# Four fused attention layers: layer 1 interleaved by batches, two result places in the heads, and a projection by seven products

## The chip, the cores and the metric

The kernel runs on one core of one Trainium2 chip. The metric is device time in microseconds of one execution, as the median of several runs; lower is better. All data are float32. The engines are named as in the profile: PE (TensorE, matmuls; PEld is its weight loads), DVE (VectorE), ACT (ScalarE), POOL (GpSimd) and SP (SyncE, which here only issues transfers and reads one flag).

## The reference, cut to what matters

Two images of 512 channels with 32 x 32 pixels pass through four layers, each of which adds to its input. Layer 0 is an attention with sampled keys and a small network for its position bias, followed by an MLP of 512 to 2048 to 512 channels. The change doesn't touch it. Layer 1 is a linear attention, layers 2 and 3 are group norm and full attention with 8 heads over 1024 positions:

```
# layer 1, n = 1024 positions, Q and K of 64 channels, V of 512
Q, K = Q / |Q|, K / |K|                       # over channels
tailor = 1 / (n + Q^T (sum_n K + eps))
x = x + gamma * (sum_n V + (V K^T) Q) * tailor

# layers 2 and 3
h = group_norm(x)
q, k, v = split(w_qkv h + b_qkv)              # 8 heads of 64 channels
a = softmax(q^T k / 8) v
x = x + (w_proj a + b_proj)                   # w_proj: 512 x 512
```

## The kernel before

The image x stays in SBUF for the whole run: `self.xs[b][t]` holds batch b, channels 128 t to 128 t + 127, as 128 partitions x 1024 positions. `CT` is 4, the number of channel tiles, `HF` is 512, half of the positions, and `DH` is 64. Weights come from DRAM by transfers on SP. The kernel is written in a framework that orders each engine's instructions by its own estimate, except inside `manual_schedule(engines=...)`: there the named engines run in the order of the text. Tiles come from pools; a tile whose buffer is still in use waits for the last reader of it. PSUM, where matmuls write, is given out in the same way.

**Layer 1** (`layer1`, L814 to L963). Queries and keys are made with positions on partitions (L844), x is transposed (L859), and norms give `qn` and `kn` (L867 to L873). Then for each batch: the sum of the keys on all partitions (`kb`, L883), x times keys (`m1`, 32 calls, L889), the key sum as a column (`s`, L900), the divisors folded into `qn` on DVE (L906 to L914), and `m`, the product with the value weights (L922), which becomes `mat` (L924). After both batches `qn` is transposed (L932), and the results `w` (L945) are added to x: for batch 0 by DVE out of PSUM (L950), for batch 1 by an ACT copy `ws` and a POOL addition (L956, L957). Only this last loop has a written order, on PE and DVE. It also makes the channel means of batch 0 for the group norm of layer 2 (`channel_means`, L1201, L1202; `group_means`, L1208 to L1219), and `norm_first` normalises the first block (`xn`).

**Queries, keys and values** of layers 2 and 3 (`queries_keys_values`) are products of 2 x 2 blocks by the scheme of seven products: `SEVEN` says for P1 to P7 which left and which right operand each multiplies, out of four blocks and three sums on either side. `left_side` has POOL make the left sums (`left_sums`, L658 to L661), `right_sums` has DVE make the right ones (L665 to L668). The MLP of layer 0 uses the same scheme.

**The heads** (`heads_bounded`) go over 16 units, unit (b, p, h): batch, pair of heads, half of the queries. A unit has eight steps n, one for each 128 keys. `score` puts 128 x 1024 logits into PSUM (L1276) and ACT takes their exp, `e` (L1280). `value` multiplies `e` with v into the unit's place `o` (L1305). The sum of the eight `e` is made by POOL (`some`, of n = 0, 1, 3, 5, L1285 and L1287) and DVE (`sum`, L1290, L1292, joined in L1294). `divide` spreads the sum over the partitions with a matmul `d` (L1322) and divides: L1327, the reciprocal L1328, L1330, L1331. The order on PE is written out: score i, then value i - 2, except that the first two values of a unit are put off to its fourth step; the division of a unit stands in the fifth step of the next one. Scores have two places in PSUM; `o` and `d` have one each:

```python
            ps_s = self.pool(ctx, f"b{k}_ps_s", 2, psum=True)
            ps_o = self.pool(ctx, f"b{k}_ps_o", 1, psum=True)
```

When a unit is done, ACT copies one half of `o` (L1314) and DVE adds the other (L1315); the result replaces the queries in `data[b][0]`.

**The projection** (`project_block`, L628) has for each batch and each of four output tiles eight calls of 128 x 128 by 128 x 512, then two DVE instructions that add bias and x (L637), and in layer 3 two stores (L639). In layer 2 one `channel_means` of layer 3 stands behind each of blocks 1 to 4, `group_means` behind blocks 5 and 6. Its weights are four tiles of their own, loaded as the heads begin (L977).

`attention` puts this together: a flag from the largest logits decides between `heads_bounded` and `heads_general`; with these inputs it is the former. While the flag is read, SP issues the loads of the next layer's weights (`meanwhile`).

Of the kernel before, what the change touches and what calls it, by code (L numbers as in the profile page):

```python
# [11 lines left out]
F32 = mybir.dt.float32  # L12
# [6 lines left out]
P = 128  # L19
# [33 lines left out]
class Net:  # L53
# [569 lines left out]
    def project_block(self, acc, att, w, bias: str, b: int, o: int, out):  # L623

        nc = self.nc
        for h in range(2):
            for t in range(CT):
                nc.tensor.matmul(  # L628
                    acc[:, h, :],
                    lhsT=w[t][:, o * P : (o + 1) * P],  # L630
                    rhs=att[t][:, h * HF : (h + 1) * HF],
                    start=(t == 0),
                    stop=(t == CT - 1),
                )
# [19 lines left out]
    def left_sums(eng, w, more):  # L654

        a11, a12, a21, a22 = (w[:, i] for i in range(4))
        s2, s3, s4 = (more[:, i] for i in range(3))
        eng.tensor_tensor(s3, a11, a21, ALU.subtract)  # L658
        eng.tensor_tensor(a21, a21, a22, ALU.add)
        eng.tensor_tensor(s2, a21, a11, ALU.subtract)  # L660
        eng.tensor_tensor(s4, a12, s2, ALU.subtract)  # L661
# [152 lines left out]
    def layer1(self, w, bias):  # L814
# [3 lines left out]
        with ExitStack() as ctx:  # L818
# [8 lines left out]
            xT, qk, qn, kn, q_at = [], [], [], [], []  # L827
# [49 lines left out]
            mats = []  # L877
            for b in range(B):


# [3 lines left out]
                kb = small.tile([P, DH + 1], F32, tag="kb", name=f"kbs{b}")  # L884
                nc.vector.tensor_scalar(kb, kb_ps, 1e-6, None, ALU.add)
                m1_ps = ps_m.tile([P, CT, DH + 1], F32, tag="m1", name=f"m1{b}")
                for t in range(CT):
# [8 lines left out]
                m1 = pool.tile([P, CT, DH + 1], F32, tag=f"m1{b}", name=f"m1s{b}")  # L896
                nc.scalar.copy(m1, m1_ps)
                s_ps = ps_m.tile([P, DH + 1], F32, tag="s", name=f"s{b}")
                for n in range(NB):
                    nc.tensor.matmul(  # L900
                        s_ps[0 : DH + 1, 0:1], lhsT=kn[b][:, n, :], rhs=ones[:, 0:1], start=(n == 0), stop=(n == NB - 1)
                    )
                ks = small.tile([DH + 1, 1], F32, tag="ks", name=f"ks{b}")
                nc.vector.tensor_copy(ks, s_ps[0 : DH + 1, 0:1])
                prod = pool.tile([P, NB, DH], F32, tag=f"prod{b}", name=f"prod{b}")
                nc.vector.tensor_tensor(  # L906
                    prod, qn[b][:, :, 0:DH], kb[:, 0:DH].unsqueeze(1).to_broadcast([P, NB, DH]), ALU.mult
                )
                d = small.tile([P, NB], F32, tag="d", name=f"d{b}")
                nc.vector.tensor_reduce(d, prod, AX.X, ALU.add)  # L910
                nc.vector.tensor_scalar(d, d, float(N), None, ALU.add)
                nc.vector.reciprocal(d, d)
                nc.vector.tensor_scalar(d, d, self.col("gamma1"), None, ALU.mult)
                nc.vector.tensor_tensor(  # L914
# [5 lines left out]
                m_ps = ps_m.tile([DH + 1, C], F32, tag="m1", name=f"m{b}")  # L920
                for t in range(CT):
                    nc.tensor.matmul(m_ps, lhsT=m1[:, t, :], rhs=w[:, t, 0:C], start=(t == 0), stop=(t == CT - 1))  # L922
                mat = pool.tile([DH + 1, C], F32, tag=f"mat{b}", name=f"mat{b}")
                nc.vector.scalar_tensor_tensor(mat, bias[0 : DH + 1, 0:C], ks, m_ps, ALU.mult, ALU.add)  # L924
                mats.append(mat)

            for b in range(B):
                for h in range(2):
                    cut = slice(h * HF, (h + 1) * HF)
# [4 lines left out]
                    nc.scalar.copy(qa, tr[0 : DH + 1, :])  # L934
                    q_at.append(qa)
            self.means_tiles(2, 0)
            self.first = {2: self.first_block(2, 0)}
            with self.tc.manual_schedule(engines={mybir.EngineType.PE, mybir.EngineType.DVE}):
                steps = self.group_means(2, 0, ps_m.tile([P, 2, CT], F32, tag="s", name="gm2"))
                for b in range(B):  # L940
# [638 lines left out]
```

## Time and profile before

| | us |
|---|---|
| median of 3 runs | 3430.6 (3429.81 to 3431.36) |
| the profiled execution | 3430.73 |
| its span, first to last instruction | 3428.9 |
| layer 1, from 2445.7 | 84.5 |
| layer 2: queries, keys, values / heads / projection | 150.1 / 241.2 / 58.4 |
| layer 3: queries, keys, values / heads / projection and end | 147.4 / 240.7 / 61.0 |

A group line of the profile has the line of the kernel, engine, operation, names of what is written and read, shape and count; then the busy time and the mean duration of one; then the engine's idle time ahead of it and what ended most of that. A timeline line begins with start and length in us, and may end with the idle time ahead and its releaser in brackets. Matmuls of float32 leave two records each, and the end of a record is modelled, so records overlap and a busy PE can hide short gaps. Stretches were cut at the first instructions of the stages.

### The profile page before, as it was taken

Reading aid. Unit: us, or ns where it says so; the run is one execution under the profiler, and the core shown is the slowest. Engines: PE = TensorE matmul, PEld = TensorE weight load, DVE = VectorE, ACT = ScalarE, POOL = GpSimd, SP = SyncE. Lnnn points to the kernel's source line nnn. Section 1 sums busy time; section 2 is a strip of 40 time slices with the busy share of each in tenths; the row PEclk is TensorE's granted clock in tenths of the full one; section 3 lists DMA queues with packets and bytes.
Section 4 is the critical chain, followed back from the end, with each engine's and each line's share of the span. In section 5 each row is a group of like instructions: output and inputs, shape, how many; then the busy total and the mean of one; then the engine's idle time right before and its main releaser. Section 6 shows DMA issues by size and latency. Waiting matters only on the chain.

```text
span 3428.9 us, 60151 instructions
## 1 busy us (share of the span) xinstructions
PE 3376.9 (98%) x25280; PEld 1243.1 (36%) x25280; DVE 2314.8 (68%) x2553; ACT 2020.2 (59%) x2102; POOL 2070.3 (60%) x1584
## 2 busy tenths in 40 slices
PE   6999999999999999999999999999999999999999
PEld 2333333333333333333333334444655433455333
DVE  6876777777776677777776664575556576555674
ACT  5887877877877688877877761111111566113661
POOL 4877777877877687878877873432324344234441
PEclk9999999999999999999999999999999999999999
DMA  5878777877877677878888861110000100000001
GB/s 152 158 150 158 158 150 153 160 151 152 160 148 146 119 158 148 167 146 156 161 165 157 161 155 63 49 49 25 1 1 6 45 2 1 1 0 13 1 1 51
DMA packets 103248, 342.65 MB, mean 100 GB/s; under 512 B 12720, under 2 KB 14384, under 8 KB 100144
## 3 DMA queue, kind: packets, MB, share of 16 engines
q0 software_dynamic: 73296, 266.90, 41.0%
q1 hardware_dynamic: 28656, 69.68, 7.1%
q8 instruction: 202, 3.31, 0.4%
q10 hardware_dynamic: 1008, 2.06, 0.2%
q14 instruction: 86, 0.70, 0.1%
HBM read 67.27 MB, written 4.46 MB: 21 GB/s over the span
## 4 chain that ended last, share of the span: by engine, by line
PE 86%; DVE 11%; ACT 1%; POOL 1%; issue 1%; DMA 0%; DVEq 0%; ACTq 0%
PE hp L515 50%; PE pb L628 3%; PE sim L547 3%; DVE r L1328 3%; PE o L1305 2%; DVE sum L1292 2%; PE s L1276 2%; PE qk20P L1071 1%; PE qk30P L1071 1%; PE m_0P L679 1%; PE qk21P L1071 1%; PE m_5P L679 1%; PE m_4P L679 1%; PE m_2P L679 1%; PE qk31P L1071 1%; PE m_6P L679 1%
## 5 line engine op out<-in xcount | busy, mean ns | idle before, releaser
L515 PE MATMUL hp<-h,w 128*32 128x512 f32 x16384 | 1822.1, 593 | 5.3 <-DVE h L484 3.6
L484 DVE CUSTOM_DVE_ANT_1 h<-tx,bank 128x1024 f32<-128x1024 f32 x1024 | 1179.9, 1215 | 276.6 <-PE hp L515 241.1
L520 ACT ACTIVATE h<-hp,magb 128x1024 f32<-128x1024 f32 x1024 | 1121.9, 1112 | 403.8 <-PE hp L515 398.8
L515 PEld LDWEIGHTS hp<-h,w 128*32 128x32 f32 x16384 | 530.4, 110 | 1221.4 <-issue 1154.3
L507 POOL DMA_DIRECT2D h<-h x509 | 451.8, 1022 | 410.4 <-ACT h L526 348.8
L533 POOL TENSOR_TENSOR h<-h,h 128x1024 f32<-128x1024 f32 x255 | 610.2, 2393 | 21.3
L531 POOL TENSOR_SCALAR h<-h,flip 128x1024 f32<-128x1024 f32 x256 | 446.9, 1746 | 0.9 <-ACT h L520 0.9
L1280 ACT ACTIVATE e<-s 128x1024 f32<-128x1024 f32 x256 | 258.4, 1024 | 177.6 <-PE s L1276 167.3
L522 ACT ACTIVATE h<-h,flip 128x1024 f32<-128x1024 f32 x256 | 291.4, 1138 | 0.0
L1305 PE MATMUL o<-e,v 64*64 64x512 f32 x2048 | 261.0, 592 | 6.9 <-DVE q L1315 6.9
L1276 PE MATMUL s<-q,k 64*64 64x512 f32 x2048 | 259.8, 589 | 2.6 <-DVE v L1109 1.8
L1287 POOL TENSOR_TENSOR some<-some,e 128x1024 f32<-128x1024 f32 x64 | 151.7, 2370 | 75.4 <-ACT e L1280 73.1
L1285 POOL TENSOR_TENSOR some<-e,e 128x1024 f32<-128x1024 f32 x32 | 75.6, 2364 | 190.9 <-DVE sum L1294 155.8
L524 POOL TENSOR_SCALAR h<-h,flip 128x1024 f32<-128x1024 f32 x128 | 144.5, 1129 | 47.9 <-ACT h L520 46.8
L526 ACT ACTIVATE h<-h,flip 128x1024 f32<-128x1024 f32 x128 | 145.6, 1138 | 0.0
L547 PE MATMUL sim<-h,ends 128*32 128x512 f32 x1024 | 142.5, 592 | 0.0
L1290 DVE TENSOR_TENSOR sum<-e,e 128x1024 f32<-128x1024 f32 x32 | 46.6, 1456 | 136.1 <-ACT e L1280 136.1
L1305 PEld LDWEIGHTS o<-e,v 64*64 64x64 f32 x2048 | 75.8, 133 | 157.4 <-issue 123.6
L1276 PEld LDWEIGHTS s<-q,k 64*64 64x64 f32 x2048 | 78.6, 133 | 143.4 <-issue 118.5
L738 ACT ACTIVATE mh<-mh,cols 128x512 f32<-128x512 f32 x64 | 46.2, 721 | 124.2 <-DVE mh L756 65.5
L658 POOL TENSOR_TENSOR mlp_w<-mlp_w 128x512 f32<-128x512 f32 x16 | 22.0, 1374 | 160.1 <-DMA mlp_w<-in_mlp_w 148.8
L1059 POOL TENSOR_TENSOR sq<-q 128x512 f32<-128x512 f32 x32 | 33.3, 1041 | 139.3 <-DVE q L1078 95.3
(463 smaller groups left out, 3278.6 us busy)
## 6 DMA issues: line engine op xcount, KB each, us to landing
h<-h POOLq DMA_DIRECT2D x509, 512.0 KB, 6.5
lb<-logs SPq DMA_DIRECT2D x63, 512.0 KB, 5.2
mlp_w<-in_mlp_w SPq DMA_DIRECT2D x16, 1024.0 KB, 4.9
x<-in_x SPq DMA_DIRECT2D x8, 512.0 KB, 9.4
qkw<-in_l_qk SPq DMA_DIRECT2D x2, 2048.0 KB, 8.2
out<-x SPq DMA_DIRECT2D x16, 256.0 KB, 2.1
vw<-in_l_v SPq DMA_DIRECT2D x2, 1024.0 KB, 7.6
proj<-in_l_proj SPq DMA_DIRECT2D x8, 256.0 KB, 5.0
```

Source lines behind the costliest of these rows:

```text
L484: self.nc.vector._custom_dve(TENSOR_ADD_SAT, out=h[:, k, :, :], in0=x[:, jj, 2 * r + k, :].unsqueeze(1).to_broadcast([P, H, W]), in1=y[:, ...
L507: nc.gpsimd.dma_start(to, what, accum_op=ALU.add)
L515: nc.tensor.matmul(hp[rows, cut], lhsT=self.l0w2[:, 32 * q : 32 * q + 32], rhs=h1[k][:, cut], start=True, stop=True)
L520: nc.scalar.activation(y, hp, AF.Relu, bias=self.magb[:, q : q + 1])
L522: nc.scalar.activation(ys[0], ys[0], AF.Copy, scale=self.flip[:, 0:1])
L531: nc.gpsimd.tensor_scalar(y, y, self.flip[:, 2:3], 1.0, ALU.mult, ALU.mult)
L533: (nc.vector if final else nc.gpsimd).tensor_tensor(y, y, ys[2], ALU.add)
L547: nc.tensor.matmul(sims[u][at : at + 32, :], lhsT=self.ends[:, 28 - 4 * o : 60 - 4 * o], rhs=z[jj][:, h * HF : (h + 1) * HF], start=(o == ...
L679: self.nc.tensor.matmul(acc[p], lhsT=w[:, a, k, p * P : (p + 1) * P], rhs=right(r, k), start=k == 0, stop=k == 1)
L1276: nc.tensor.matmul(s[halves[c], par, :], lhsT=ks[p][rows, at : at + DH], rhs=qs[p][rows, cut], start=True, stop=True)
L1280: nc.scalar.activation(e, s, AF.Exp, scale=DH**-0.5)
L1305: nc.tensor.matmul(o[halves[par], r, :], lhsT=v[n // 2][rows, n % 2, at : at + DH], rhs=e[rows, par, :], start=(n == 0), stop=(n == NB - 1),)
```

## The change

Four things are changed.

1. Layer 1. From the key sums on, the order is written out for PE, ACT and DVE. Batch 0 runs through to its `mat` first; its results are then made in turn with `m1` of batch 1 (two results, one channel mean, a quarter of `m1`), and the rest of batch 1 follows. `group_means` and `norm_first` stand among the results of batch 1.
2. Heads. PSUM now has four places, "a", "b", "even" and "odd". Scores take "a" and "b" in turn; `o` and then `d` of a unit take "even" or "odd" by its h. The values always follow two steps behind the scores. The order is written out for PE, DVE and POOL.
3. Projection. It becomes seven products of 256 x 256 by 256 x 512 for each batch. The left sums, and the right sums but three, are made by POOL during the heads of batch 1, two or three in the seventh step of a unit; the last three are made by DVE behind the last division. In P7 and P5 POOL adds to x.
4. Weights. The values' weights are loaded as the layer begins, and the projection's weights as one load into the same buffer, ahead of the reading of the flag. In memory they are stored by blocks.

```diff
     @staticmethod
     def left_sums(eng, w, more):
-        eng.tensor_tensor(s3, a11, a21, ALU.subtract)
...
+        for step in Net.left_steps(eng, w, more):
+            step()
...
     def layer1(self, w, bias):
...
+            engines = {getattr(mybir.EngineType, e) for e in ("PE", "Activation", "DVE")}
+            with self.tc.manual_schedule(engines=engines):
+                keys_sum(0)
+                for _ in divisors(0):
+                    pass
+                for _ in keys_x(0):
+                    pass
+                keys_column(0)
+                turned(0)
+                matrix(0)
+                keys_sum(1)
+                divided, summed = divisors(1), keys_x(1)
+                for t in range(CT):
+                    for h in range(2):
+                        result(0, h, t)
+                    self.channel_means(2, 0, t)
+                    next(summed)
+                    if t in (0, 2):
+                        next(divided, None)
+                next(summed, None)
+                keys_column(1)
+                turned(1)
+                matrix(1)
                 steps = self.group_means(2, 0, ps_m.tile([P, 2, CT], F32, tag="s", name="gm2"))
+                next(steps)
+                for h in range(2):
+                    for t in range(CT):
+                        result(1, h, t)
+                        if h == 0 and t == 2:
+                            next(steps, None)
+                        elif h == 1 and t == 1:
+                            self.norm_first(2)
...
     def queries_keys_values(self, k, wpool, weights, ones, data):
...
             with self.tc.manual_schedule(engines={mybir.EngineType.SP}):
-                got = meanwhile()
+                got = self.attention_weights(wpool, 3, "qk") if k == 2 else None
+                proj = self.attention_weights(wpool, k, "proj")
...
     def heads_bounded(self, k, ones, data, proj, out):
...
+            places = {x: self.pool(ctx, f"b{k}_ps_{x}", 1, psum=True) for x in ("a", "odd", "even", "b")}
...
-                third = unit is units[0] and n == 2
-                s = (ps_o if third else ps_s).tile([P, 2, HF], F32, tag="sd"[third], name=f"s{k}{b}{p}{h}{n}")
+                at = {0: "b", 1: "a", 2: "odd"}.get(n) if unit is units[0] else None
+                s = place(at or ("a", "b")[n % 2], f"s{k}{b}{p}{h}{n}")
...
-                    state["o"] = ps_o.tile([P, 2, HF], F32, tag="o", name=f"o{k}{b}{p}{h}")
+                    state["o"] = place(home(h), f"o{k}{b}{p}{h}")
...
-                d = ps_o.tile([P, 2, HF], F32, tag="d", name=f"d{k}{b}{p}{h}")
+                d = place(home(h), f"d{k}{b}{p}{h}")
...
+            for b in range(B):
+                att = data[b][0]
+                r = [[att[2 * (i // 2) + c][:, (i % 2) * HF : (i % 2 + 1) * HF] for c in range(2)] for i in range(4)]
+                if b == 0:
+                    t = [x.rearrange("p (c x) -> p c x", c=2) for x in data[0][1]]
+                else:
+                    t = data[0][2]
+                t1, t2, t3, t4 = ([x[:, c, :] for c in range(2)] for x in t)
+                right.append([r[0], t3, r[2], r[3], t1, t2, t4])
+                if b == 1:
+                    sums += self.left_steps(nc.gpsimd, proj, more)
+                    sums += [subtract(nc.gpsimd, t1[c], r[1][c], r[0][c]) for c in range(2)]
+                for c in range(2):
+                    eng, to = (nc.vector, late) if b == c == 1 else (nc.gpsimd, sums)
+                    if b == 0:
+                        to.append(subtract(eng, t1[c], r[1][c], r[0][c]))
+                    to.append(subtract(eng, t2[c], r[3][c], t1[c]))
+                    to.append(subtract(eng, t3[c], r[3][c], r[1][c]))
+                    to.append(subtract(eng, t4[c], r[2][c], t2[c]))
...
+                at = ("a", "b", "even", "a", "b", "even", "a") if b == 0 else ("odd", "even", "b", "odd", "even", "a", "b")
+                for which, spot in zip(("P1", "P3", "P2", "P6", "P7", "P5", "P4"), at):
...
+                        if which == "P1":
+                            nc.scalar.copy(u, got)
+                            add(vec, p, 0, got, True)
+                        elif which == "P3":
+                            add(vec, p, 1, got, True)
+                        elif which == "P2":
+                            add(vec, p, 0, got)
+                            store(p, 0)
+                        elif which == "P6":
+                            vec.tensor_tensor(u, got, u, ALU.add)
+                        elif which == "P7":
+                            u3 = u3s[:, p, :]
+                            vec.tensor_tensor(u3, got, u, ALU.add)
+                            add(pool, p, 3, u3)
+                            if p == 1:
+                                for q in range(2):
+                                    add(pool, q, 2, u3s[:, q, :])
+                        elif which == "P5":
+                            vec.tensor_tensor(u, got, u, ALU.add)
+                            add(pool, p, 1, u)
+                            store(p, 1)
+                            add(vec, p, 3, got, True)
+                            store(p, 3)
+                        else:
+                            add(vec, p, 2, got, True)
+                            store(p, 2)
+                    yield
...
-                for i in range(len(steps) + 5):
+                for i in range(len(steps) + 2):
                     if i < len(steps):
                         score(*steps[i])
-                    for j in ([], [i - 3, i - 2])[i % NB == 3] if i % NB in (2, 3) else [i - 2]:
...
+                    if i >= 2:
+                        value(*steps[i - 2])
                     if i % NB == 4 and NB < i < len(steps):
                         divide(steps[i - NB][0])
...
+                    if i % NB == 6 and i > len(steps) // 2 + NB:
+                        for _ in range(3 if i < len(steps) * 3 // 4 else 2):
+                            sums.pop(0)()
+                for n, _ in enumerate(project(0)):
+                    if n == 2:
+                        divide(units[-1])
+                        for do in late:
+                            do()
+                for n, _ in enumerate(project(1)):
+                    if k == 2:
+                        if n < 2:
+                            self.channel_means(3, 0, 2 * n)
+                            self.channel_means(3, 0, 2 * n + 1)
+                        elif n == 2:
+                            means = self.group_means(3, 0, place("a", "gm3"))
+                            next(means)
+                        elif n == 3:
+                            next(means, None)
+                            self.norm_first(3)
```

`add(eng, p, i, what)` adds a result to block i of x, `store` sends a block of the output in layer 3, and `left_steps` gives the four left sums one by one.

## The prediction

> **What bounds the kernel.** First the busy times and the chain of waits.
>
> ```profile
> span 3428.9 us, 60151 instructions
> PE 3376.9 (98%) x25280; PEld 1243.1 (36%) x25280; DVE 2314.8 (68%) x2553; ACT 2020.2 (59%) x2102; POOL 2070.3 (60%) x1584
> PE 86%; DVE 11%; ACT 1%; POOL 1%; issue 1%; DMA 0%; DVEq 0%; ACTq 0%
> ```
>
> TensorE is the bound, so matmuls taken out shorten the span one for one, and only gaps on PE matter. The change leaves layer 0 and its MLP alone; its stages lie behind 2445.7 us. Busy time by stretch shows them: layer 1; then for layers 2 and 3 queries/keys/values, heads, projection.
>
> ```profile
> 2445.70:2530.20 84.50, 78.04 (x472) 56.36 (x471) 40.71 (x78) 14.66 (x27) 31.87 (x25) 0.93 0.00 1
> 2680.30:2921.50 241.20, 236.35 (x2169) 81.33 (x2169) 165.47 (x138) 146.40 (x159) 113.69 (x48) 1.00 0.03 10
> 2921.50:2979.90 58.40, 56.85 (x145) 24.83 (x141) 27.07 (x46) 4.02 (x6) 9.66 (x4) 1.00 0.01 1
> 3368.00:3429.00 61.00, 56.35 (x137) 24.30 (x136) 19.91 (x24) 1.17 (x2) 0.00 (x0) 1.00 0.19 70
> ```
>
> (Columns: length; busy PE, PEld, DVE, ACT, POOL; granted clock; DMA.) Layer 1 alone has a clock below 1.00. The projections are dense; the heads look so, but records of matmuls overlap, so a busy PE hides short gaps. The timeline of one unit shows them, PE first, then DVE, then GpSimd (POOL):
>
> ```profile
> 2838.33 1.04 PE L1322 MATMUL d<-sum,ones 64*64 64x512 f32 x8
> 2847.77 1.90 PE L1276 MATMUL s<-q,k 64*64 64x512 f32 x16
> 2849.91 1.95 PE L1305 MATMUL o<-e,v 64*64 64x512 f32 x16 [0.24 <-DVE q L1315]
> 2853.39 1.04 PE L1322 MATMUL d<-sum,ones 64*64 64x512 f32 x8
> ...
> 2838.80 1.42 DVE L1290 TENSOR_TENSOR sum<-e,e 128x1024 f32<-128x1024 f32 x1 [4.01 <-ACT e L1280]
> 2848.03 1.23 DVE L1294 TENSOR_TENSOR sum<-sum,some 128x1024 f32<-128x1024 f32 x1
> 2849.17 0.68 DVE L1315 TENSOR_TENSOR q<-o,q 128x512 f32<-128x512 f32 x1
> ...
> 2836.78 2.37 POOL L1287 TENSOR_TENSOR some<-some,e 128x1024 f32<-128x1024 f32 x1
> 2849.40 2.36 POOL L1285 TENSOR_TENSOR some<-e,e 128x1024 f32<-128x1024 f32 x1 [5.57 <-DVE sum L1294]
> ```
>
> The unit's new o has no place until L1315 has emptied the old one. From d to d a unit takes 15.06 us.
>
> **Heads, two places.** A step's score and its value start 0.858 us apart (neighbouring rows, 2835.76 to 2837.47). A unit is 8 scores, 8 values, one d: 17 x 0.858 = 14.59. So each boundary loses 0.47, and 15 boundaries a layer 7.0 us (the idle column shows half). With o alternating between "even" and "odd", the first value of a unit needs a place whose last d was read ten steps before; the wait goes. d moves into its own o's place, a new wait for L1315, but that ended at 2849.85 and d came at 2853.39: 3.5 us of cover. Scores keep two places, as before; exp takes 1.02 of a 1.72 us step. Gain 7.0 a layer.
>
> **Heads, the sums on GpSimd.** 17 additions of 128x512 are queued behind the unit's third "some" (7 units, 3 or 2 each). The nearest rows are L1111 and L797: 1.25 to 1.27 us. POOL sat idle 5.57 there, so by busy time they are free. Against that: L1290 above took 1.42 and not 1.22, since it began while POOL's L1287 ran to 2839.15; another, begun with 0.99 of one left (2689.60), took 2.07. [...] The bounds are 0 and 4.3; I take 1.0 a layer, near the rows. Heads: 2 x (7.0 - 1.0) = 12.0.
>
> **Projection, seven products.** L628 has 256 records for 128 calls, 111.4 us; a block of 8 calls repeats after 6.87 us (L637 at 3390.06, 3396.93), 0.858 a call. Seven products with 4 calls are 28 calls a batch against 32: 16 fewer in two layers, 13.7 us, 6.87 a layer. VectorE's evictions of a batch are 16 at 0.7, with the last division (4 ops, 5.2 us) and three late sums (0.7) 18.5 of 24.0 us on PE. The tightest place is "a" for P4: P6's eviction queues behind division and late sums to about 20.6 after the start, P4 is due at 21.5. No stall, 0.9 of cover.
>
> Layer 2 adds one. gm3's matmul now stands behind P2 of batch 1, and needs four channel_means. After P1 VectorE has two evictions (1.41), two means (1.52 each), P3's evictions, two means: 0.2 + 1.4 + 3.0 + 1.4 + 3.1 = 9.2 us, PE is there after P3 and P2, 6.9. PE waits 2.4, P6 and all behind it too. Before, one mean lay under each 6.87 us.
>
> Does that wait also cost clock? Windows of 2 us in layer 1 (PE busy, clock):
>
> ```profile
> 2513.00:2515.00 2.00, 1.71 (x5) 1.00 0.00 0
> 2515.00:2517.00 2.00, 1.32 (x4) 1.00 0.02 4
> 2519.00:2521.00 2.00, 2.00 (x3) 0.50 0.00 0
> 2533.00:2535.00 2.00, 2.00 (x4) 0.50 0.00 0
> ```
>
> Two gaps of under 1 us sufficed there to halve the clock, from about 2518.3 to 2535.3. [...] A single gap of 1.55 (start of layer 3) cost none. [...] Layer 2: 6.87 - 2.4 - 1.7 = 2.8.
>
> Layer 3's tail: before, the last store was issued right behind L637's last eviction. Now P7's and P5's six GpSimd additions (1.25 each) end 1.5 after PE, and behind the store that waits for them stand three more on SP, 0.44 apart (the four proj loads took 1.75): 1.2 later. [...] proj's 256 KB landed in 5.0 when four were issued together, a store in 2.1. Between 0 and 2.9; I add 1.0, since the first two will be gone. 6.87 - 2.2 = 4.7.
>
> **Layer 3's start.** proj goes into v's buffer, so layer 3's v loads behind the projection (landing 7.6, first read by left_side(1) at 13.7 or later: covered). SP's proj load ahead of the branch waits for the last values, as vw's load did in layer 2 before, where PE waited 0.88 at the branch as in layer 3 without one: nothing. But left_side(0), 4 x 2.4 us, which POOL ran at 2936 to 2946 under the old projection, now stands behind its additions, and starts 1 us into layer 3, beside right_sums on VectorE (4 x 1.23, from 3.3 us on)[...]: ready at about 13.9, P3 needs it at 13.7. I count 0.5; 0 to 2.
>
> **Layer 1.** Before: w's 16 calls run from 2507.1 to 2527.1, 14.2 us by count; then PE waits 2.9 for xn, and starts layer 2 at half clock until 2535.3. After, counted with the rows (kb 1.73, m 7.15, s 0.9, four transposes 0.5, matrix 3.43, w 0.86): transposes end at 2480.5 as before (VectorE bounds them); batch 0: 1.7 + 7.2 + 0.9 + 1.0 + 3.4 = 14.2; kb of batch 1 1.7; four rounds of two w and a quarter of m, 3.5 each, 14.0 (VectorE 2 x 0.69 + 1.52 = 2.9 each, and 2.7 for the divisors: 14.3, with three places to run ahead); s, transposes, matrix 5.3; mat's own 0.74 uncovered, 0.9; eight w and gm 7.1. Sum 43.2, end 2523.7. norm_first runs under the last two w, but L1219, L1227 and L1228 may each wait for a GpSimd addition: 0.8. Layer 2 starts at 2524.5, not 2530.2: 5.7; with the clock whole, half of 5.1 us of slow matmuls comes back: 2.5. Gain 8.2. It would be 9.9 if batch 0's kb still slipped between the transposes as before, and 0 if the rounds stall enough to halve the clock again.
>
> **Sum.** 12.0 + 2.8 + 4.7 - 0.5 + 8.2 = 27.2, against the profiled execution, 3430.73 (its span 3428.9 and 1.8 around it); the median of the runs is 3430.6, no correction. 3430.7 - 27.2 = 3403.5.
>
> **Rivals.** All covers hold ([...]no clock loss, stores not queued; for it: POOL's 5.57 idle): 14.0 + 4.5 + 6.9 + 8.2 = 33.6, 3397. Chance 0.20. [...]4.3 a layer (for it: L1290's 1.42 and 2.07[...]): 6.6 less, 3410. 0.18. Layer 1 gains nothing (against: its PE work is 65 of the 76 us behind the MLP's last matmul): 3412. 0.10. The heads gain nothing, another wait taking L1315's place (against: ACT is idle 0.6 to 0.7 before each exp): 3415.5. 0.05. Slower: every GpSimd sum lengthens the unit in full, because L1285 of the next unit waits for L1294 and "some" has one buffer: 34 x 1.25 = 42.5 against 29.2 gained otherwise, 3444; it decides from 0.86 us per sum on. Against it: 5.57 idle for three sums of 3.75. 0.03. Gains and losses level within 0.2% (6.9 us, about what this kernel's measurement can tell from no change): 0.02. The rest, 0.42, is my forecast.
>
> Range 3394 to 3414: it takes in the forecast and the first three rivals with their bounds. Faster 0.95, same 0.02, slower 0.03.
>
> **What would show it.** L1305's idle time <-DVE L1315 near 0 and d every 14.6 us in units 0 to 8; later units up to 1 us longer, PE d waiting for sum or q, L1290 to L1294 over 1.3 us. pb with 224 records and 97.5 us. One PE wait of 2.4 at gm for mv in layer 2, with a stretch at 0.50 behind it. left_side(0) of layer 3 behind its first matmul. Layer 1 from the MLP's last matmul to qk20P in 70 us, not 76, without the half clock. Wrong if heads stay at 240 us, or PE waits for POOL anywhere by over 5 us.

## The result, and the profile after

| | us |
|---|---|
| before, on the same chip | 3430.64 (3429.81 to 3431.36) |
| after, median | 3411.19 (3410.49 to 3412.34) |
| ratio | 0.9942, 95% interval 0.9931 to 0.9953 |
| after, the profiled execution / its span | 3411.19 / 3409.2 |

The change saves 19.5 us, where 27.2 were forecast; 3411 lies near the upper end of the range, 3394 to 3414. The head of the page first: busy times, and the chain of waits in shares.

```profile
span 3409.2 us, 60195 instructions
PE 3354.4 (98%) x25248; PEld 1246.9 (37%) x25248; DVE 2417.5 (71%) x2591; ACT 2026.5 (59%) x2109; POOL 2172.1 (64%) x1642
PE 90%; DVE 6%; POOL 2%; ACT 1%; DMA 1%; issue 1%; DVEq 0%; ACTq 0%; POOLq 0%; SPq 0%
```

PE has 22.5 us less to do (3376.9 before), and the span fell by 19.7. VectorE and GpSimd are each busier by 102 us: part of it is added work, part is that the same instruction takes longer (L1337: 1.22 us at the least, 3.27 at the most; L1290, its like in before: 1.23 to 2.07). The stages in the same order as before: layer 1, the heads of layer 2, its projection, and layer 3's projection with the end (length; busy PE, PEld, DVE, ACT, POOL; granted clock; DMA).

```profile
2444.00:2524.90 80.90, 76.33 (x479) 56.27 (x478) 42.65 (x78) 14.67 (x28) 28.54 (x23) 1.00 0.00 1
2672.40:2910.80 238.40, 234.48 (x2170) 82.14 (x2169) 199.84 (x136) 148.18 (x159) 147.75 (x64) 1.00 0.02 6
2910.80:2967.40 56.60, 51.86 (x129) 22.47 (x125) 42.37 (x67) 6.25 (x10) 17.94 (x15) 0.97 0.02 4
3351.60:3409.20 57.60, 49.54 (x124) 21.31 (x120) 35.30 (x45) 3.52 (x6) 17.58 (x14) 0.95 0.20 75
```

Layer 1 has its clock whole. Layer 2's projection has not: 0.97. (The 0.95 of the last stage lies behind PE's end.) In the heads VectorE is busy for 199.84 us, 34 more than before, with no instruction of its own added there. Cut at the same instructions of PE in both traces, the ledger is this:

| stage, by PE | before | after | difference |
|---|---|---|---|
| up to the MLP's last matmul (unchanged) | 2454.26 | 2455.57 | +1.3 |
| layer 1, to the first matmul of layer 2 | 75.94 | 69.38 | -6.6 |
| layer 2, queries to first score | 150.90 | 147.43 | -3.5 |
| layer 2, heads | 240.36 | 238.39 | -2.0 |
| layer 2, projection | 58.41 | 56.61 | -1.8 |
| layer 3, queries to first score | 148.34 | 147.39 | -0.9 |
| layer 3, heads | 239.73 | 236.82 | -2.9 |
| layer 3, projection and end | 60.96 | 57.61 | -3.4 |

So the heads, with 12.0 the largest part of the forecast, gave 4.9. The list of PE's waits (total, times, longest) has the new ones:

```profile
PE d L1369 <- DVE q L1362: 5.7, 8, 1.2
PE gm L1247 <- DVE mv L1241: 3.0, 1, 3.0
PE qk30P L1109 <- DVE x L1417: 1.8, 1, 1.8
PE qk20P L1109 <- ACT ws L968: 1.3, 1, 1.3
```

Two of the waits of before are gone, the one for a place of `o` and the one of each layer's first score:

```profile
PE o L1305 <- DVE q L1315: 6.9, 28, 0.6
PE s L1276 <- DVE v L1109: 1.8, 2, 0.9
```

L1352, the value matmul of after, has 0.8 us of idle time ahead of it in all. In its stead PE waits at `d`. The timeline shows two units, an early one and one in which GpSimd makes three sums. PE first, the last value and the `d` behind it:

```profile
2751.66 1.04 PE L1352 MATMUL o<-e,v 64*64 64x512 f32 x8
2752.52 1.04 PE L1369 MATMUL d<-sum,ones 64*64 64x512 f32 x8
...
2855.49 1.04 PE L1352 MATMUL o<-e,v 64*64 64x512 f32 x8
2857.73 1.09 PE L1369 MATMUL d<-sum,ones 64*64 64x512 f32 x8 [1.20 <-DVE q L1362]
```

The early `d` comes 0.86 us behind the value, as every step should. The late one comes 2.24 behind it: 1.4 lost. The list of waits says 1.2, since the value's record ends late. DVE over the late unit, then POOL:

```profile
2841.57 3.07 DVE L1337 TENSOR_TENSOR sum<-e,e 128x1024 f32<-128x1024 f32 x1
2844.56 0.68 DVE L1374 TENSOR_TENSOR r<-d,r 128x512 f32<-128x512 f32 x1
2845.27 3.35 DVE L1375 RECIPROCAL r<-r 128x512 f32<-128x512 f32 x1
2848.66 1.21 DVE L1377 TENSOR_TENSOR q<-q,r 128x512 f32<-128x512 f32 x1
2849.90 1.38 DVE L1378 TENSOR_SCALAR q<-q,cols 128x512 f32<-128x512 f32 x1
2851.21 4.54 DVE L1339 TENSOR_TENSOR sum<-sum,e 128x1024 f32<-128x1024 f32 x2
2855.85 1.23 DVE L1341 TENSOR_TENSOR sum<-sum,some 128x1024 f32<-128x1024 f32 x1
2856.99 0.68 DVE L1362 TENSOR_TENSOR q<-o,q 128x512 f32<-128x512 f32 x1
...
2841.20 2.36 POOL L1332 TENSOR_TENSOR some<-e,e 128x1024 f32<-128x1024 f32 x1 [2.56 <-DVE sum L1341]
2843.64 5.68 POOL L1334 TENSOR_TENSOR some<-some,e 128x1024 f32<-128x1024 f32 x2
2849.27 1.73 POOL L1388 TENSOR_TENSOR k<-q,q 128x512 f32<-128x512 f32 x1
2850.96 1.47 POOL L1388 TENSOR_TENSOR k<-q,k 128x512 f32<-128x512 f32 x1
2852.38 2.28 POOL L664 TENSOR_TENSOR projm<-projw 128x512 f32<-128x512 f32 x1
```

VectorE has no pause in this unit: it is a chain of its own. Four of its lines run long beside GpSimd's additions: L1337 1.23 alone, here 3.07; L1377 0.69, 1.21; L1378 0.49, 1.38; the two of L1339 2.55, 4.54. That is 5.2 us on top of 10.9, and makes a unit of 16.0 from `d` to `d`, against the 14.59 that PE needs. Read from `d` to `d`, the units of layer 2 take 14.59 as long as no sums are there, then 14.82, 16.00, 16.02 (three sums each), 15.11, 15.14, 14.91 (two each): 4.5 over; layer 3 likewise 4.0 over.

### The profile page after: what moved, and what is told of

Same layout as the page of the kernel before. It is cut to its first block, busy times and chain, and to the rows that moved or that the text cites. A ratio compares the mean times of both kernels' runs of the same rounds, so it can differ in the third digit from the quotient of the medians.

```text
span 3409.2 us, 60195 instructions
## 1 busy us (share of the span) xinstructions
PE 3354.4 (98%) x25248; PEld 1246.9 (37%) x25248; DVE 2417.5 (71%) x2591; ACT 2026.5 (59%) x2109; POOL 2172.1 (64%) x1642
## 4 chain that ended last, share of the span: by engine, by line
PE 90%; DVE 6%; POOL 2%; ACT 1%; DMA 1%; issue 1%; DVEq 0%; ACTq 0%; POOLq 0%; SPq 0%
PE hp L515 50%; PE s L1323 5%; PE o L1352 5%; PE sim L547 3%; PE qk20P L1109 1%; PE qk30P L1109 1%; PE m_0P L686 1%; PE m_6P L686 1%; PE m_3P L686 1%; PE m_2P L686 1%; PE m_1P L686 1%; PE qk31P L1109 1%; PE qk21P L1109 1%; PE m_5P L686 1%; PE m_4P L686 1%; PE m_7P L686 1%
## 5 line engine op out<-in xcount | busy, mean ns | idle before, releaser
L1352 PE MATMUL o<-e,v 64*64 64x512 f32 x2048 | 267.7, 589 | 0.8 <-ACT e L1327 0.8
L1323 PE MATMUL s<-q,k 64*64 64x512 f32 x2048 | 267.9, 589 | 0.0
L1332 POOL TENSOR_TENSOR some<-e,e 128x1024 f32<-128x1024 f32 x32 | 75.6, 2364 | 171.7 <-DVE sum L1341 138.7
L1334 POOL TENSOR_TENSOR some<-some,e 128x1024 f32<-128x1024 f32 x64 | 166.8, 2607 | 24.9 <-ACT e L1327 21.2
L1352 PEld LDWEIGHTS o<-e,v 64*64 64x64 f32 x2048 | 83.4, 133 | 137.4 <-issue 132.2
L1337 DVE TENSOR_TENSOR sum<-e,e 128x1024 f32<-128x1024 f32 x32 | 79.5, 2484 | 64.0 <-ACT e L1327 63.9
L1375 DVE RECIPROCAL r<-r 128x512 f32<-128x512 f32 x32 | 107.3, 3353 | 1.1
```

The lines of the kernel that those rows point to most:

```text
L1323: nc.tensor.matmul(s[halves[c], par, :], lhsT=ks[p][rows, at : at + DH], rhs=qs[p][rows, cut], start=True, stop=True)
L1352: nc.tensor.matmul(o[halves[par], r, :], lhsT=v[n // 2][rows, n % 2, at : at + DH], rhs=e[rows, par, :], start=(n == 0), stop=(n == NB - 1),)
```

## The experiments

### What lengthens the units: the sums, their reading, or their time

In `e1_no_sums` the 17 additions of a layer in the heads of batch 1 are left out, and one memset stands for what they write; in `e2_memset` each becomes a memset of 128 x 1536, 1.42 us, longer than the addition. Both therefore compute something else in the projection.

```diff
-                            sums.pop(0)()
+                            sums.pop(0)            # e1: left out
...
+                            nc.gpsimd.memset(more, 0.0)   # e2: in each one's place
```

> The changed kernel with the 17 sums that GpSimd makes in the heads of either layer left out (one memset stands in for the left sums). Theory A: the waits of PE at d in units 9 to 15 (4.5 us a layer) come from these sums[...]. Then d comes every 14.59 us in all units, the heads take 233.8 us instead of 238.4 and 236.8, and the time is 3411.2 - 8 to 9 = 3402 to 3403. Theory B: the loop of VectorE and GpSimd is itself 15.06 us long (as L1339 to L1339 is in units 4 to 7) and runs out of cover with or without the sums: then units 9 to 15 come at 15.0, and the time is 3407 or more.

> In place of each of the 17 sums GpSimd runs a memset of 128x1536 (about 1.5 us by the 0.52 of the 128x512 memset in layer 1), which takes as much of GpSimd's time or more but reads nothing from SBUF. Theory A[...]: no waits at d, 3402 to 3403 as without the sums, L1337 and L1339 not longer than without them. Theory C (GpSimd's time: the unit's next additions stand behind the sums in its queue): waits at d as in the changed kernel or longer, 3411 or more.

Measured: e1 3402.03 (3401.55 to 3402.72), ratio to before 0.9912 (0.9895 to 0.9928); e2 3401.74 (3401.69 to 3401.99), 0.9911 (0.9894 to 0.9927). In both every unit takes 14.59, and PE never waits at `d`. In the heads alone e1 is 4.5 and 4.0 below after. So the sums cost some 8.5 us in the two layers, and not by GpSimd's time, of which e2 uses more. e2's timeline, DVE then POOL, in a unit with three memsets:

```profile
2846.91 2.54 DVE L1339 TENSOR_TENSOR sum<-sum,e 128x1024 f32<-128x1024 f32 x2
...
2845.33 4.41 POOL L1489 MEMSET projm<- 128x1536 f32 x3
```

The two additions of L1339 take 2.54 beside a GpSimd that writes without a break, as alone; beside a GpSimd that adds, they took 4.54. So it is GpSimd's additions that lengthen L1339, and its memsets don't.

### Is the sums' price due to "some" having one buffer?

The rival that ended on the slower side said that the sums delay the next unit's L1332, because "some" has one buffer. `e3_two_some` gives it two.

```diff
-state["some"] = ap.tile([P, 2, HF], F32, tag="some", name=...)
+state["some"] = ap.tile([P, 2, HF], F32, tag="some", bufs=2, name=...)
```

> The changed kernel with two buffers for some, so that GpSimd's first addition of a unit need not wait for the last of VectorE's additions of the unit before. If the single buffer is what makes the loop of both engines 15.06 us long (B), cover is not used up in units 1 to 8 and the sums find 3.5 us of it: some 3 us a layer come back, 3405. [...]1 us or less comes back in all: 3410 to 3411.

Measured: 3428.23 (3424.91 to 3435.11), ratio 0.9992 (0.9985 to 0.9998): nearly all of the change's gain is gone, which no theory had. The heads of the profiled execution are 7.6 and 8.1 longer than after's; three stretches of 3.4 us at half clock behind the new waits are in that, about 5 us. The line of PE's waits:

```profile
PE d L1369 <- DVE q L1362: 16.6, 10, 3.5
```

And the end of a unit in the timeline, on DVE and then POOL:

```profile
2841.32 4.50 DVE L1339 TENSOR_TENSOR sum<-sum,e 128x1024 f32<-128x1024 f32 x2
2845.93 3.20 DVE L1341 TENSOR_TENSOR sum<-sum,some 128x1024 f32<-128x1024 f32 x1
...
2845.12 2.93 POOL L1332 TENSOR_TENSOR some<-e,e 128x1024 f32<-128x1024 f32 x1 [0.38 <-ACT e L1327]
2848.63 2.74 POOL L1334 TENSOR_TENSOR some<-some,e 128x1024 f32<-128x1024 f32 x1 [0.58 <-ACT e L1327]
```

With one buffer GpSimd's L1332 can't begin before VectorE's L1341 has read `some` (in after it starts at 2841.20, released by L1341). With two it starts at 2845.12, ahead of L1341, which then takes 3.20 and not 1.23. Units with sums take up to 18.3. The single buffer is no bottleneck here: it holds GpSimd back just where VectorE has the last two instructions that PE waits for.

### Taking VectorE's division into PSUM

In the late unit of after, L1337, L1339, L1377 and L1378 ran long, and all of them read SBUF alone; L1362 and L1374, which have one operand in PSUM, kept their 0.68, and the reciprocal its 3.35. In `e8_div_psum` reciprocal and product go to `d`'s place in PSUM, so that L1377 and L1378 have an operand there.

```diff
-                nc.vector.reciprocal(t, t)
-                nc.vector.tensor_tensor(res, res, t, ALU.mult)
-                nc.vector.tensor_scalar(res, res, self.col(f"vb{k}", p), None, ALU.add)
+                nc.vector.reciprocal(d[:, 0, :], t)
+                nc.vector.tensor_tensor(d[:, 1, :], res, d[:, 0, :], ALU.mult)
+                nc.vector.tensor_scalar(res, d[:, 1, :], self.col(f"vb{k}", p), None, ALU.add)
```

> The kernel after with three steps of the division[...]: reciprocal and product are written to d's place in PSUM, so that the product and the bias addition have one operand in PSUM each. Theory A[...]: units with sums fall from up to 16.0 to under 15.2, the heads from 238.4 and 236.8 to about 234.5: 3411.2 - 5 = 3406, or 3403 if all waits at d go. Rival B (the division's place in the loop is idle time anyway, since VectorE waits there for the next e): 3410 to 3412. Rival C (d's place is held longer and o's next matmuls wait for it): over 3412.

Measured: 3403.03 (3401.64 to 3403.18), ratio 0.9917 (0.9901 to 0.9934), 8.2 less than after and about 1 us above leaving the sums out; in the heads alone it is 0.3 and 0.1 above e1. A unit with three sums, on DVE:

```profile
2846.61 0.70 DVE L1377 TENSOR_TENSOR d<-q,d 128x512 f32<-128x512 f32 x1
2847.34 0.75 DVE L1378 TENSOR_SCALAR q<-d,cols 128x512 f32<-128x512 f32 x1
2848.01 3.79 DVE L1339 TENSOR_TENSOR sum<-sum,e 128x1024 f32<-128x1024 f32 x2
```

L1377 and L1378 keep 0.70 and 0.75 beside GpSimd's additions (1.21 and 1.38 in after), though L1378 alone was quicker out of SBUF (0.49). The longest unit is 14.80. L1339 still runs long, 3.79 and not 2.55; it no longer matters.

### Spreading the sums

`e7_spread` and `e11_spread` leave the sums as they are and place them otherwise: the four left sums one each in units 2 to 5, the others two each in units 8 to 12 and one or two in the last ones. In e7 one subtraction of batch 1 (`t2`) stands in unit 13, ahead of the division whose result it reads, and so reads another value; in e11 it stands behind it.

```diff
...
+                    if i % NB == 6 and 2 <= i // NB < 6:
+                        lefts.pop(0)()
-                    if i % NB == 6 and i > len(steps) // 2 + NB:
-                        for _ in range(3 if i < len(steps) * 3 // 4 else 2):
+                    if i % NB == 6 and i // NB >= B * CT:
+                        for _ in range((2, 2, 2, 2, 2, 0, 1, 2)[i // NB - B * CT]):   # e7: 2, 2, 2, 2, 2, 1, 1, 1
                             sums.pop(0)()
```

> The kernel after with the 17 GpSimd additions of a layer spread: the four that need only the first load come one each in units 2 to 5, two each in units 8 to 12, one each in units 13 to 15, instead of three in units 9 to 11 and two in 12 to 15. Same additions, same number. Theory A (each unit with sums runs over by its own amount, since the loop of VectorE and GpSimd is already 15.06 us without them and TensorE's 14.59 eats its lead in eight units: the price is set by the number of sums, each about 0.6 us): units 2 to 5 have lead to pay with, so about 4 x 0.6 = 2.4 a layer less in the late units, some 1 to 2 of it back by the lead that the early ones use up: 3408 to 3411. Theory B (only the excess over a slack counts[...]): [...]3403. Rival C (the earlier sums spoil later units as much as they spare): 3411 to 3413.

> The kernel after with the spreading alone: four additions in units 2 to 5, two each in units 8 to 12, one in unit 14, two in unit 15, each behind all that it reads (in the run e7_spread one addition of batch 1 stood a unit ahead of the division whose result it reads). Theory A (three additions in one unit cost 1.4 us each of nine times a unit's TensorE time, two cost 0.3 to 0.5, one nothing): heads at 234.6 and 233.7, as in e7_spread, 6.9 us less than after: 3404.3. Rival B (the addition that waits costs more where it stands now): 3406 to 3408.

Measured: e7 3404.76 (3404.15 to 3408.69), ratio 0.9923 (0.9907 to 0.9940); e11 3406.13 (3403.56 to 3408.59), 0.9923 (0.9907 to 0.9938). The heads are 234.6 and 233.7 in both, 6.9 us less than after: nearest to theory B of e7, and what theory A of e11 had. So the price isn't so much per sum: the unit's excess over what lead is left counts. e11's own time is 5.1 below after, not 6.9, and so lies where its rival B had put it, though not by that rival's cause, since the heads are as short as theory A said. Its four executions took 3403.6, 3403.9, 3408.3 and 3408.6; the profiled one is the longest, and its clock shows what probably took the rest (windows of 2 us, columns as above):

```profile
2513.00:2515.00 2.00, 1.19 (x6) 0.60 (x5) 0.99 (x4) 0.00 (x0) 0.00 (x0) 1.00 0.00 0
2519.00:2521.00 2.00, 2.00 (x3) 0.76 (x3) 1.89 (x4) 0.58 (x1) 1.82 (x3) 0.50 0.00 0
2529.00:2531.00 2.00, 2.00 (x4) 0.73 (x3) 1.28 (x5) 1.91 (x3) 0.00 (x0) 0.50 0.03 8
```

Layer 1 is the same here as in after, with the same gap of 0.81 at `w`; yet in the profiled executions of e7 and e11 the clock fell behind it, in e11 from 2517.5 to 2531.1, and in after's it did not. Half of 13.6 would be 6.8 us; as PE is idle in part of the stretch, layer 1 and the queries of layer 2 together take 5.8 longer than in after.

### The parts by themselves: places alone, and the old layer 1

`e5_places` is the kernel before with the four places and the steady order of the heads alone; `e6_old_layer1` is after with layer 1 in its old order.

```diff
+            places = {x: self.pool(ctx, f"b{k}_ps_{x}", 1, psum=True) for x in ("a", "odd", "even", "b")}
...
-                    for j in ([], [i - 3, i - 2])[i % NB == 3] if i % NB in (2, 3) else [i - 2]:
-                        if 0 <= j < len(steps):
-                            value(*steps[j])
+                    if i >= 2:
+                        value(*steps[i - 2])
```

> The kernel before with one part of the change alone: four single places in PSUM, o alternating between two of them, d in its own o's place, scores first in three places, and the steady order of scores and values. Old layer 1, old projection of eight products, no sums on GpSimd in the heads. Theory A (the prediction's term: 15 boundaries of 0.47 us, 7.0 a layer, plus the start of the heads, 0.88 a layer, which the trace after shows gone): 3430.6 - 14.0 - 1.8 = 3414.9, d every 14.59 us in all units. Theory B (part of those 7.0 came from elsewhere[...], their loop being 15 us long): 3418 to 3425, with waits of TensorE at d. Rival C (places gain nothing by themselves): 3430.

> The kernel after with layer 1 put back to its order before. Theory A (the whole of the stage's 6.6 us and of the 2.6 us of half clock at the start of layer 2 come from the interleaving): 3411.2 + 9.1 = 3420.3, with a clock of 0.50 for some 17 us around the end of layer 1. Theory B (the clock's fall was not of layer 1's making): 3411.2 + 6.6 = 3417.8, the clock 1.00 throughout. Rival C (the new layer 1 only trades places with a wait in layer 2's start): under 3415.

e5: 3417.06 (3415.35 to 3417.29), ratio 0.9958 (0.9941 to 0.9975), 14.2 less than before, 15.8 expected by theory A. The units are 14.59 but for the last, 14.9; heads and projection together are shorter by 6.3 and 6.7, and the stages before them, queries to first score, by 1.1 and 0.9. Layer 1, which is that of before, takes 1.8 longer here, its stretch of half clock being 20.5 and not 17.1 us; that is enough for what is missing from the 15.8. Theory B falls: without the sums there is no wait at `d`. e6: 3419.66 (3418.77 to 3420.39), ratio 0.9966 (0.9953 to 0.9978), 8.5 more than after, 9.1 expected; its clock is 0.50 from about 2516.4 to 2536.9, and its layer 2 starts at 2531.6, not 2525.0. So the interleaving carries both parts of layer 1's gain.

### The wait at the group means

`e4_means_later` moves `group_means` of layer 3 one product later in layer 2's projection.

```diff
-                        elif n == 2:
+                        elif n == 3:
                             means = self.group_means(3, 0, place("a", "gm3"))
                             next(means)
-                        elif n == 3:
+                        elif n == 4:
```

> The changed kernel with both steps of group_means in layer 2's projection one product later (behind P6 and P7 of batch 1). The wait of 3.0 us at gm goes, since VectorE has 3.4 us more; without it the granted clock stays at 1.00, which gives back the 1.7 us of one window at half speed: 3411.2 - 4.7 = 3406.5. If the clock falls for another reason, or the norm of layer 3's first block now comes late: 3408 to 3411.

Measured: 3408.24 (3407.48 to 3408.70), ratio 0.9929 (0.9912 to 0.9946), 3.0 less than after, where 4.7 were expected. The wait of 3.0 is gone, and with it the 3.4 us at 0.50 that followed it in after; a new one of 1.3, which the expectation did not have, comes at P5, whose place "a" the means hold until L1255:

```profile
2955.52 7.13 PE L1437 MATMUL pb21P<-v,projw 128*128 128x512 f32 x16 [1.33 <-DVE sc L1255]
```

The stage is 53.26 instead of 56.61: 3.0 of wait and 1.7 of clock less, 1.3 more. Layer 1, the same in both, takes 1.7 longer in this trace: its clock is at 0.50 from 2509.7 to 2513.1, ahead of the gap at `w`.

### Put together

Three kernels join the edits: `e9_three` the division in PSUM, the means one product later with P5 in place "b" and P4 in "a", and the last P5 addition of layer 3 on VectorE; `e10_four` also the spreading of e11; `e12_four_b` is e10 with P5 and P4 where e4 had them.

```diff
-... ("odd", "even", "b", "odd", "even", "a", "b")    # e4, e12
+... ("odd", "even", "b", "odd", "even", "b", "a")    # e9, e10
...
-                            add(pool, p, 1, u)
+                            add(vec if out is not None and b == 1 else pool, p, 1, u)
```

> The kernel after with three edits: the division's reciprocal and product written to d's place in PSUM (as measured alone: 8.2 us less than after); group_means one product later, with P5 of batch 1 in place b and P4 in place a, so that P5 has no wait for the means' place; the last P5 addition to x of layer 3 on VectorE instead of GpSimd. Theory A (the three act on different stages and add up): 3403.0 - 4.3 (3.0 of wait at gm and 1.7 of half clock, or the 3.0 measured and the new wait of 1.3 undone) - 1.4 (one GpSimd addition of 1.25 and one store less behind it): 3397.3. Rival B (the tail is SP's six stores at 0.58 each, whatever the last addition's engine): 3398.5. Rival C (P5 and P4 with exchanged places wait elsewhere, by as much as the wait undone): 3400.

> The kernel of the run before in this call with a fourth edit: the 17 GpSimd additions of a layer spread, four in units 2 to 5, two each in units 8 to 12, one in unit 14, two in unit 15. Theory A ([...]the units with three additions still run over by 0.4 us in the two layers together, 0.21 the most in a unit; spread, none does): 0.4 less than the run before. Rival B (nothing is left to gain there): the same within 0.3. Rival C (additions in early units take the lead of the units behind): 1 to 2 more.

> The kernel of e10_four with P5 of batch 1 back in place a and P4 in place b (as in e4_means_later): the means' place is then waited for at P5 (1.3 us in e4_means_later), and layer 3 starts with a wait of 1.8 us, not 3.0 as in e9_three and e10_four, where a clock of 0.50 followed for one window. Theory A (time is lost by one long gap and the clock's fall behind it, and the same idle time in two shorter gaps costs no clock): 1.7 to 2.3 us less than e10_four, 3398.3, and no half clock between 2940 and 2990 us. Rival B (the clock falls on the sum of the idle time, whatever its pieces): the same as e10_four within 0.5.

| | us | ratio to before |
|---|---|---|
| e9_three | 3400.91 (3399.05 to 3408.41) | 0.9914 (0.9901 to 0.9928) |
| e10_four | 3400.34 (3399.67 to 3401.19) | 0.9909 (0.9894 to 0.9924) |
| e12_four_b | 3398.47 (3397.54 to 3406.20) | 0.9911 (0.9898 to 0.9925) |

e9 is 3.6 above what its theory A had. P5's wait is gone in e9 and e10, but the one at layer 3's start has grown from 1.8 to 3.0, and the clock falls behind it: so the exchanged places wait elsewhere, as rival C said. e9's wait, and its windows of 2 us around it:

```profile
PE qk30P L1109 <- DVE x L1417: 3.0, 1, 3.0
```

```profile
2956.00:2958.00 2.00, 0.00 (x0) 0.00 (x0) 2.00 (x5) 0.00 (x0) 2.00 (x2) 1.00 0.52 94
2958.00:2960.00 2.00, 1.06 (x2) 0.58 (x3) 0.69 (x2) 1.85 (x3) 0.06 (x1) 0.77 0.98 406
2960.00:2962.00 2.00, 2.00 (x3) 0.80 (x3) 1.47 (x5) 0.37 (x1) 0.00 (x0) 0.50 0.10 41
2962.00:2964.00 2.00, 2.00 (x5) 0.84 (x4) 1.97 (x3) 0.69 (x1) 1.96 (x1) 0.87 0.01 4
```

In e12 there are two waits:

```profile
PE qk30P L1109 <- DVE x L1417: 1.8, 1, 1.8
PE pb21P L1437 <- DVE sc L1255: 1.3, 1, 1.3
```

PE's idle time is the same, 3.0 in one piece or 1.3 and 1.8; only the one piece is followed by a half clock, of 3.4 us by the shares in e9's windows; e12's clock stays at 1.00 from 2940 to 2990. Layer 3's queries take 149.1 in e9, 149.9 in e10 (which waits another 0.5 for a left sum of GpSimd's), and 147.4 in e12. The tail is 1.1 to 1.7 shorter in the three than in after. e12 came to within 0.2 us of what theory A gave, 1.9 below e10, and 12.7 below after, the best of all; its median and e10's are nearer than the ranges are wide, so that step rests on the stage and its clock. In e10 and e12 no unit of the heads exceeds 14.6, and their heads are 0.4 shorter than e9's, as expected of the spreading.

## Why the prediction was right, and where it was not

The direction and the range held, and so did the mechanisms, but for the price of the sums. That 3411 still lies in the range is owed to its upper end, which was drawn to take in the rivals: the heads of layer 2 took 238.4, nearer to the 240 that the prediction named as a sign of being wrong than to the 234 that it forecast. The 7.5 us that are missing from the forecast are nearly one term, the price of the sums, which was too small by a factor of four; the errors of the others, three up and four down, come to about 1 us.

| term | forecast | measured |
|---|---|---|
| heads, two places | 14.0 | 13.4 (e1's heads against before's, 6.5 and 6.9) |
| heads, their start | 0 | 1.8 (0.9 a layer) |
| heads, sums on GpSimd | -2.0 | -8.5 (after against e1) |
| projection of layer 2 | 2.8 | 1.8 |
| projection of layer 3 and end | 4.7 | 3.4 |
| layer 3's start | -0.5 | 0 |
| layer 1, with its clock | 8.2 | 9.1 |
| unchanged part, run to run | 0 | -1.3 |
| sum | 27.2 | 19.7 |

**The sums: the step that failed.** "The bounds are 0 and 4.3; I take 1.0 a layer, near the rows." It was 4.5 and 4.0. Its upper bound, 4.3, was the author's estimate and was not shown by before's trace, where L1290 took 1.42 and 2.07 in place of 1.22. Two of layer 2's three units with three sums took 16.0, and units with two 14.9 to 15.1, against 14.59 without. What the 1.0 missed is that such delays add up in one engine's serial chain: in the late unit above L1337, begun with 1.99 of GpSimd's L1332 left, took 1.84 longer, L1377 0.52, L1378 0.89 and the two of L1339 1.99. L1378, a TENSOR_SCALAR with a single tensor input, gave no warning: its like in before, L1331, took 0.49 all 32 times.

And the cover was not 3.5. That was read between L1315's end and `d` in a kernel whose rhythm of 15.06 was set by the very wait that the change removes. At 14.59 the lead of L1362 over `d` goes down by about 0.47 a unit, and back up by 1.5 whenever L1337 gets in ahead of a GpSimd addition: in e1 it moves between 2.76 and 1.05 once the first units are past. At the last `d` ahead of the sums it stood at 1.25 in layer 2 and at 2.74 in layer 3. Lead and loss together are what the units ran over: 5.7 in layer 2 and 6.6 in layer 3. So the rival with 4.3 a layer and 3410 came nearest to the outcome, but by luck, since the cover was not the 3.5 that the prediction had read.

**Two places.** Right: 0.47 a boundary, in e5 alone and inside after. The 0.9 at the start of each layer's heads had been seen in the trace ("PE waited 0.88 at the branch"), but only to ask whether a load adds to it. It went with the new places, in e5 as well: the first score no longer stands behind the last eviction of v, which in after begins at 2672.49, when that score (2672.38) is under way.

**The projection.** Seven products gave their 6.87 a layer less the waits. The wait at the means was 3.0, not 2.4: VectorE's second eviction of P1 stood 0.65 for ACT's copy, which the count of VectorE's own work left out. The clock fell behind it, as the rows of layer 1 suggested; that it would cost 1.7 was the author's estimate, which before's trace doesn't show: its only stretch at 0.50 lasts 17.1 us. The windows of after around it:

```profile
2947.00:2949.00 2.00, 0.00 (x0) 0.00 (x0) 1.97 (x5) 0.00 (x0) 0.00 (x0) 1.00 0.00 0
2949.00:2951.00 2.00, 1.44 (x3) 0.93 (x4) 1.90 (x7) 0.00 (x0) 0.00 (x0) 0.61 0.00 0
2951.00:2953.00 2.00, 2.00 (x4) 0.93 (x3) 0.28 (x2) 0.00 (x0) 0.00 (x0) 0.54 0.00 0
```

From the shares, 0.50 holds from about 2949.4 to 2952.8, 3.4 us, of which half is lost. 6.87 - 3.0 - 1.7 is 2.2; 0.2 of the 0.4 by which layer 2 gave less is the wait ahead of layer 3's first matmul, 1.77 and not 1.55; the rest isn't placed.

**The tail.** It cost 3.5, not 2.2. PE's last matmul, GpSimd's last six additions and SP's stores in after:

```profile
3394.11 7.03 PE L1437 MATMUL pb31P<-v,projw 128*128 128x512 f32 x16
...
3395.14 4.95 POOL L1419 TENSOR_TENSOR x<-x,pv 128x512 f32<-128x512 f32 x4 [14.75 <-DVE pv L1459]
3400.05 2.48 POOL L1419 TENSOR_TENSOR x<-x,pu 128x512 f32<-128x512 f32 x2
...
3401.34 3.50 SPq L1425 DMA_DIRECT2D out<-x  x6
```

All six stores, and not four, stand behind the first addition of P5, and issue 0.62 apart, not 0.44; the span ends 8.1 behind PE, against 4.5 before. With the last P5 addition on VectorE (e12) the stores start at 3388.0, ahead of PE's end at 3389.7, and the span ends 6.4 behind it.

**Layer 1 and layer 3's start.** `kb` of batch 0 did slip in between the transposes; for that case the forecast had 9.9, and 9.1 came. That the clock stayed whole behind the new layer 1 is in part luck: in three of the eleven traces that have it, 13.6 us of half clock followed (last section). The 0.8 for additions of GpSimd had a likeness in before's trace: L1219, on 128 x 4, took 1.01 at 2528.1, where an addition of L957 ran to 2529.1, and 0.16 the three other times. The left sums of layer 3 were late as foreseen, but PE didn't wait for them; the 13.9 was an estimate.

## What to carry to other kernels

Slack that is read from a trace belongs to that trace's rhythm: when a change removes the wait that sets the rhythm, work out the slack again at the new pace before work is laid into it. An engine that is idle by its busy time isn't free if its work lengthens the instructions of a serial chain on another, as GpSimd's additions did with VectorE's (L1339 from 2.55 to 4.54); here spreading such work over units with a lead of their own took 6.9 us off the heads, and taking VectorE's operands into PSUM gave 8.2 us for three changed lines. A wait that can't be removed may cost less in two pieces than in one: in e10 3.0 us were followed by 3.4 at half clock, in e12 1.3 and 1.8 by none. More buffers can be worse: the one buffer of `some` was what kept GpSimd off VectorE's last instructions.

## What the runs showed of the hardware that was not expected

- A VectorE TENSOR_SCALAR of 128 x 512 from SBUF to SBUF took 1.38 us beside GpSimd's additions and 0.49 alone (L1378 in after); with its input in PSUM it took 0.75 all 32 times (e8). Slower by itself, it was quicker in such company.
- A small instruction ran long too: L1266 and L1267, on 128 x 4, took 1.19 in e4, where they came under GpSimd's additions of P7, and 0.16 in after.
- Beside GpSimd's memsets VectorE's L1339 took 2.53 to 2.54 for two, as alone, but L1378 took up to 1.14 (e2).
- The stretches at 0.50 differed in length. Behind the wait of 3.0 in layer 2's projection it was 3.41 us (after); the stretches that begin in layer 1 measure 3.4 (e4, e8), 13.6 (e3, e7, e11), 17.1 (before) and 20.5 us (e5, e6). Eleven traces have the same gap of 0.81 us in the same order of matmuls in layer 1: in e3, e7 and e11 13.6 us of half clock followed; in the other eight the `w` behind it ran at full clock. What tells these cases apart was not shown.
- From layer 2 on, PE's wait of 3.0 was followed by half clock in e9 and e10 (at layer 3's start) and, at `gm`, in after, e1 and e11 by their clock and in e2 and e3 by the matmuls' pace; the waits of 1.3 and 1.8 in e4 and e12, with seven us of matmuls between them, were not. Of four waits of 3.4 to 3.5 at `d` in e3 three were, and one (`d` at 3283.84) was not: the steps behind it start 0.86 apart. In layer 1 the gap of 0.81, or in before 0.29 and 0.68, could be enough, and in e4 the clock fell ahead of the gap. What else counts stays open.
